# A relational graph layer on one core: row fetches with counters of their own, narrower first halves, later place transposes

## The chip, the cores and the metric

The kernel runs on one core of a Trainium2 chip. A core has five engines that run side by side, each with its own list of instructions in a fixed order, and that wait for one another through semaphores: TensorE (PE), which multiplies matrices and keeps its results in PSUM; VectorE (DVE) and ScalarE (ACT) for elementwise work; GpSimd (POOL), which here issues gathers; and SyncE (SP), which issues transfers. ACT issues transfers too. The metric is the device time of one execution in microseconds (us). The profile is that of one more execution.

## The reference

There are N = 12,500 nodes with 256 features each and E = 212,500 edges, sorted by destination; the last edge of each node is its loop to itself. Each edge has one of 8 types. What is computed:

```python
h = maximum(layernorm(x), 0)
hx = einsum('ni,rio->rno', h, weight)              # 8 weights of 256 x 256
agg = segment_sum(hx[edge_type, src], dst)         # sum over the edges into each node
out = x + agg * 0.5**0.5 + h_bias + (h @ loop_weight) * 0.5**0.5
```

All of it is float32. The kernel sums first and multiplies later: for each node and type it sums the rows h[src] of the edges, and multiplies the eight sums by the eight weights.

## The kernel before

**Units and tiles.** The sorted edge list is cut into 792 units. A unit holds up to 256 edges without their loops, as two tiles of 128 edges; there are 1583 tiles, numbered t. For a tile the kernel needs the 128 rows h[src], one to a partition (`msg`), and a one-hot matrix `oh` that says for each edge which column (destination within the unit's window of 22 nodes, times 8 types) it goes to. PE multiplies the two (`edge_sums`, line 883): the message rows are the stationary operand, in two halves of 128 features, and the one-hots move. One such product is two instructions in float32, so a tile is four pairs of weight load and matmul. A unit's second half of slots is multiplied first, over 22 x 8 = 176 columns; its first half (odd t) over `REACH[0][1]` x 8 = 16 x 8 = 128 columns, up to block 6, in which both take 176. DVE then adds the unit's sums to a ring of columns in SBUF at an offset that it has loaded into a register (`add_sums`, line 897); four PSUM banks take turns.

**Groups.** 128 nodes are a group; there are 98. When the last unit that can touch a group has been added, its 18 products with the weights (line 1070, 36 instructions of 256 columns) are queued and spread over the tiles that follow, from `ready` to `until`. `finish` (line 1082) adds the result to x and stores four groups at a time. It then prepares the ring slot six groups on: `begin` transposes that group's own rows (line 924) and writes its loop edges through eight DVE instructions (line 942). At every fourth group it queues `find_types`: a search on PE (line 975), a chain of DVE steps (lines 981 to 994) and a spread on PE (line 1002).

**Order of work.** The whole program is written in one order by the loop over t: at step t it issues the gather of tile t + 64, up to `FETCH` row fetches on SP and as many on ACT, one-hots a few tiles ahead, the tile's matmuls, and small jobs. Jobs that need the one shared PSUM bank `pt` go through `shared`: a first part on PE, then DVE parts two tiles later. A job may not run before the tile at which it was queued plus `wait`, nor while another one is active. Each engine then takes its instructions in that order and waits where data is missing.

**Blocks.** 128 units are a block. Its edge lists are prepared 232 tiles ahead in small steps: loads on SP, eight small loads of spans by ACT (line 363), and from 20 tiles later one DVE step per tile (lines 416 to 660). These compact the lists, transpose them on PE (line 372) and end in `places`: positions in the ring are computed on DVE (line 659) and transposed on PE (line 664). `verdict` checks after the last block (line 679) that every edge found a column; all engines read its flag, and a general path follows only if one did not.

**Messages.** A gather is one indirect transfer of 128 rows by POOL (line 818). `msgs` holds 66 tiles, so a tile's buffer is free once PE has read the tile 66 before it. From block 1 on, every 36th tile (t % 36 = 35, tiles 287 to 1511, 35 of them) is not gathered: SP and ACT fetch its rows one by one. `gather` queues four chunks of 32 rows, in turn for SP and ACT, from 8 tiles later. A chunk (`load_sources`) first loads 32 row numbers into registers (line 825), then issues 32 transfers of 1 KB each (line 831):

```python
for i, v in reversed(list(enumerate(vals))):
    fetches[engine].insert(0, (0, lambda i=i, v=v: queue.dma_start(
        msg[t][r0 + i : r0 + i + 1, :].bitcast(U8),
        h32_bytes[:, bass.ds(v, D * 4)])))
```

The framework gives each transfer of SP and ACT one of eight semaphores in turn. The next transfer that gets the same semaphore waits for the one before, whichever of the two engines issued it, and PE waits for all eight before it reads a fetched tile.

Of the kernel before, what the change touches and what calls it, by code (L numbers as in the profile page):

```python
# [11 lines left out]
U8 = mybir.dt.uint8  # L12
# [6 lines left out]
SYNC_DEP = mybir.DependencyInfo(mybir.DependencyClass.Sync, mybir.DependencyReason.DATA)  # L19
DVE = mybir.EngineType.DVE  # L20
SP = mybir.EngineType.SP
ACT = mybir.EngineType.Activation

P = 128
# [15 lines left out]


WIN = 22
REACH = ((0, 16), (0, 22))

GROUP = 128

# [4 lines left out]
MSGS = 66  # L51
AHEAD = 64

SINGLE = 36
FETCH = 3
SOURCES = 32
HOLD = 8


QUAD = 4  # L60
# [8 lines left out]
SOON = 8  # L69
# [9 lines left out]

PREP = 232  # L80
LOADED = 20
SHARE = 1.15
OVERDUE = 24

# [143 lines left out]
def kernel(  # L228
# [11 lines left out]
    nc = tc.nc  # L240
# [9 lines left out]
    U = PAIR * P  # L250
# [42 lines left out]
    with ExitStack() as main:  # L293
# [30 lines left out]
        firsts, stops, loops, marked, typed, gidx, col = {}, {}, {}, {}, {}, {}, {}  # L324
        added, zeroed = {}, {}
        single, fetches = {}, {SP: [], ACT: []}
        state = {"h32": None}


# [37 lines left out]
        def turned(got, cols, to):  # L367

            def turn():
                for i in range(PAIR):  # L370
                    half = slice(i * P, (i + 1) * P)
                    nc.tensor.transpose(pt[:, half], got[cols][:, half], ident)  # L372

            return [lambda: shared(turn, [(2, lambda: nc.vector.tensor_copy(to(), pt[:, :U]))])]

        def work_tile(got, name, tag, dtype=F32):
            got[name] = ep.tile(
# [268 lines left out]
        def places(b, got):  # L646

            def wraps_():
                got["wrapped"] = small.tile([P, NK], F32, name="wrapped")
                nc.vector.tensor_scalar(  # L650
                    got["wrapped"], wraps, got["base"][:, 0:1], None, op0=ALU.is_lt)

            def turns():
                got["turns"] = small.tile([P, 1], F32, name="turns")
                nc.vector.tensor_reduce(got["turns"], got["wrapped"], AX.X, ALU.add)

            def position():
                got["pos"] = small.tile([P, 1], F32, name="pos")
                nc.vector.scalar_tensor_tensor(
                    got["pos"], got["turns"], float(-RING), got["base"][:, 0:1],  # L660
                    op0=ALU.mult, op1=ALU.add)

            def turn():
                nc.tensor.transpose(pt[0:1, :P], got["pos"], ident)

            def keep():
                place[b] = small.tile([1, P], I32, name="offs")
                nc.vector.tensor_copy(place[b], pt[0:1, :P])

            return [wraps_, turns, position, lambda: shared(turn, [(2, keep)])]  # L670

        def verdict(got):

            def count():
                got["count"] = small.tile([P, 1], F32, name="count")
                nc.vector.tensor_reduce(got["count"], counts, AX.X, ALU.add)

            def total():
                nc.tensor.matmul(pt[0:1, 0:1], got["count"], ones, start=True, stop=True)  # L679

            def differs():
                nc.vector.tensor_scalar(flag, pt[0:1, 0:1], float(E), None, op0=ALU.not_equal)

            def compare():
                shared(total, [(2, differs)])

            def load():
                state["general"] = nc.values_load(flag[0:1, 0:1], min_val=0, max_val=1)

            return [count, compare, load]  # L690
# [5 lines left out]
        def shared(first, then, ready=lambda: True, wait=0):  # L696

            if done["tile"] is None:
                first()
                for _, f in then:  # L700
                    f()
                return
            jobs.append((first, list(then), ready, done["tile"] + wait, done["step"]))
# [94 lines left out]
        def gather(t):  # L798
            if t % PAIR == 0:
                both = msgs.tile([P, PAIR, D], F32, name="msg")  # L800
                for i in range(PAIR):
                    msg[t + i] = both[:, i, :]
            if t % QUAD:
                kind[t] = kind[t - 1]
            else:
                kind[t] = "h" if state["h32"] is not None and t >= state["h32"] + LATE else "x"
            table = {"h": h32, "x": x}[kind[t]]
            b, i, u = place_of(t)
            if b and t % PAIR and kind[t] == "h" and t + AHEAD < NT:
                if t % SINGLE == SINGLE - 1:  # L810
                    for k, r in enumerate(range(0, P, SOURCES)):
                        engine = ACT if k % 2 else SP
                        fetches[engine].append((
                            done["tile"] + HOLD,
                            lambda r=r, engine=engine: load_sources(t, r, engine)))
                    return
            at = i * P + u
            nc.gpsimd.indirect_dma_start(  # L818
                out=msg[t], out_offset=None, in_=table[:, :],
                in_offset=bass.IndirectOffsetOnAxis(ap=gidx[b][:, at : at + 1], axis=0))  # L820

        def load_sources(t, r0, engine):

            b, _, u = place_of(t)
            _, vals = nc.values_load_multi_w_load_instructions(
                single[b][u : u + 1, r0 : r0 + SOURCES], engines=[engine],
                min_val=0, max_val=(N - 1) * D * 4,
                skip_runtime_bounds_check_because="clamped to the table where they are computed")
            queue = {SP: nc.sync, ACT: nc.scalar}[engine]
            for i, v in reversed(list(enumerate(vals))):  # L830
                fetches[engine].insert(0, (0, lambda i=i, v=v: queue.dma_start(
                    msg[t][r0 + i : r0 + i + 1, :].bitcast(U8),
                    h32_bytes[:, bass.ds(v, D * 4)])))

        def fetch(n):
            for list_ in fetches.values():
# [31 lines left out]
        def edge_sums(t):  # L868
            m, o = msg.pop(t), oh.pop(t)
            if t % PAIR == 0:  # L870
                bank = banks[t // PAIR % BANKS]
                sums["ps"] = bank[:, : KC * R * WIN].rearrange("p (c k) -> p c k", c=KC)
            ps = sums["ps"]
            i = t % PAIR
            width = R * (REACH[0][1] if i and t // (PAIR * P) < NB - 1 else WIN)
            end = t == NT - 1 or i == PAIR - 1
            free = added.get(t // PAIR - BANKS)
            if i == 0 and free is not None and latest["pe"] is not None:
                tc.add_manual_dep(latest["pe"], free.name, SYNC_DEP, reason="bank is free")
            if i == 0 and latest["pe"] is not None:  # L880
                tc.add_manual_dep(latest["pe"], made[t], SYNC_DEP, reason="one-hots are made")
            for c in range(KC):
                j = nc.tensor.matmul(  # L883
                    ps[:, c, :width], m[:, c * P : (c + 1) * P], o[:, :width],
                    start=(i == 0 and c == 0), stop=(end and c == KC - 1))
            latest["pe"] = j.ins
            return ps

        sums = {}
# [77 lines left out]
        def find_types(q):  # L967
# [37 lines left out]
                typed[q] = types.tile([P, XG * GROUP], BF16, name="types")  # L1005
                nc.vector.tensor_copy(typed[q], pt)

            shared(spread, [(2, types_of)], lambda: q in marked, wait=2)

        got = {}  # L1010

# [103 lines left out]
        with tc.manual_schedule():  # L1115
# [111 lines left out]
            for t in range(NT):  # L1227
# [57 lines left out]
                while waiting and (len(waiting) > LAG or t == NT - 1):  # L1285
                    u, ps = waiting.pop(0)
                    add_sums(u, ps)
                    while (next_group < plan.NG and plan.last[next_group] <= u
                           and (done["weights"] or (NT <= 400 and done["norm"] == len(pieces)))):
                        g = next_group  # L1290
                        while background and NT <= 400:
                            step()
                        until = PAIR * (plan.first[g + SLOTS] - 3) - REST if g + SLOTS < plan.NG else NT - 1
                        ready = t + max(0, min(DELAY, NT - 1 - t - 2 * DELAY))
                        until = max(ready, min(until, ready + int(GROUP / plan.rate * PAIR)))
                        if g >= plan.NG - SOON:
                            until = min(until, ready + DELAY)
                        if g and g % SLOTS == 0:
                            wrap(g)
                        work = [] if g else group_ahead(0)  # L1300
                        work += group_work(g)
                        if g + 1 < plan.NG:
                            work[-8:-8] = group_ahead(g + 1)
                        for c, f in work:
                            queue.append((ready, until, c, f))
                        next_group += 1
# [36 lines left out]
```

## Time and profile before

| | us |
|---|---|
| median of 3 runs (2461.66 to 2462.48) | 2462.18 |
| the profiled execution | 2461.46 |
| its span, first to last instruction | 2459.7 |
| PE busy with matmuls | 1914.6 (78%) |
| DVE busy | 1385.7 (56%) |
| POOL busy | 1474.6 (60%) |
| ACT busy (issues not counted) | 143.5 (6%) |

The page gives busy time by engine, the same in 40 slices of the span with the clock that PE was granted, and groups of instructions by source line with the mean duration of one and the idle time just before it. PE stands for matmuls, PEld for the weight loads that run beside them. A row of the waits says which engine's instruction waited for what: total us, times, longest. "issue" is idle time in which the profile shows nothing that was waited for; "remote" is a semaphore whose raiser it could not name. A line of the timeline has the start in us, the duration, the engine, the source line, the operation, and a count where several were merged. "ACTq" and "SPq" are issues of transfers by ACT and SP, which do not count as busy. A table of stretches gives for each the busy time and number of instructions of an engine, the granted clock and what the transfers moved.

### The profile page before, as it was taken

What the parts mean: (1) busy time and instruction counts of PE and PEld (TensorE: products, weight loads), DVE (VectorE), ACT (ScalarE), POOL (GpSimd) and SP (SyncE); (2) the same over time, 40 slices, a digit from 0 to 9 for tenths busy, and PEclk for the clock granted to TensorE, in tenths of its full rate; (3) what the DMA queues carried; (4) which work ended last, traced back from release to release, by engine and by line L of the source; (5) the groups of instructions that cost most, each with busy time, mean ns of one, the idle gap of its engine ahead of it and who ended that gap; (6) DMA issues with size and microseconds to landing.
All of it is one profiled execution on the core that took longest, in us unless ns stands there. A gap on an engine that the chain in (4) does not pass through costs nothing. (4 is left out here: it accounts for less than half of the span.)

```text
span 2459.7 us, 38134 instructions
## 1 busy us (share of the span) xinstructions
PE 1914.6 (78%) x10339; PEld 1679.8 (68%) x10339; DVE 1385.7 (56%) x3530; ACT 143.5 (6%) x267; POOL 1474.6 (60%) x1574
## 2 busy tenths in 40 slices
PE   0157888888888877888888788788888888878889
PEld 0146677777777767777777677677777677777788
DVE  3387735446754546755455765455765445765453
ACT  3474300000000000000000000000000000000000
POOL 7535666666666666666666666666666666666630
PEclk9558998989998999898999999999899999999999
DMA  6584433343333333333333333334333333333320
GB/s 203 165 295 132 124 93 116 90 125 106 101 114 106 100 116 109 103 107 97 117 107 106 116 106 99 108 99 123 108 99 114 109 96 108 117 99 117 110 73 13
DMA packets 155220, 279.46 MB, mean 114 GB/s; under 512 B 33679, under 2 KB 105464, under 8 KB 155000
## 3 DMA queue, kind: packets, MB, share of 16 engines
q0 software_dynamic: 74304, 203.00, 27.8%
q1 hardware_dynamic: 74616, 71.68, 9.3%
q10 hardware_dynamic: 6080, 2.31, 0.4%
q8 instruction: 82, 1.34, 0.2%
q14 instruction: 138, 1.13, 0.1%
HBM read 251.26 MB, written 25.60 MB: 113 GB/s over the span
## 5 line engine op out<-in xcount | busy, mean ns | idle before, releaser
L818 POOL DMA_INDIRECT msg<-h,gidx x1448 | 1377.8, 952 | 815.6 <-issue 354.3
L883 PE MATMUL ps<-oh,msg 128*128 128x176 f32 (+1 forms) x6332 | 1191.2, 315 | 326.7 <-issue 177.4
L883 PEld LDWEIGHTS ps<-oh,msg 128*128 128x128 f32 x6332 | 1079.1, 206 | 474.8 <-issue 283.8
L1070 PE MATMUL po<-w,acc 128*128 128x256 f32 x3136 | 945.6, 402 | 113.0 <-issue 102.5
L897 DVE TENSOR_TENSOR acc<-acc,ps 128x352 f32 x792 | 408.9, 516 | 700.1 <-remote 364.0
L1070 PEld LDWEIGHTS po<-w,acc 128*128 128x128 f32 x3136 | 564.5, 201 | 206.3 <-issue 166.2
L850 DVE TENSOR_TENSOR oh<-fixed,cols 128x704 f32<-128x704 f32 x397 | 349.0, 880 | 0.0
L942 DVE SCALAR_TENSOR_TENSOR acc<-types,pt 128x256 f32<-128x256 bf16 (+1 forms) x688 | 248.9, 412 | 105.2 <-remote 54.6
L818 POOL DMA_INDIRECT msg<-in_x_dram,gidx x100 | 94.8, 948 | 83.5 <-issue 46.4
L1070 PE MATMUL po<-wl,self_t 128*128 128x256 f32 x392 | 113.3, 408 | 13.9 <-issue 7.9
L1070 PEld LDWEIGHTS po<-wl,self_t 128*128 128x128 f32 x392 | 71.8, 204 | 26.7 <-issue 13.6
L1082 DVE TENSOR_TENSOR xr<-xr,po 128x256 f32<-128x256 f32 x98 | 40.5, 413 | 32.4 <-PE po L1070 14.7
L772 ACT ACTIVATE msg<-msg,e_shift,e_rstd 128x256 f32<-128x256 f32 x100 | 51.8, 589 | 21.5 <-DVE e_shift L769 10.2
L772 ACT ACTIVATE xt<-xt,n_shift,n_rstd 128x256 f32<-128x256 f32 x98 | 50.9, 589 | 21.6 <-DVE e_stats L760 7.0
L924 PE MATMUL pt<-ident,hr 128*128 128x128 f32 x196 | 41.8, 292 | 12.7 <-issue 9.4
L1083 DVE TENSOR_TENSOR xr<-xr,po 128x256 f32<-128x256 f32 x98 | 41.2, 421 | 4.4 <-DVE xr L1082 1.1
L929 DVE COPY self_t<-pt 128x256 f32<-128x256 f32 x98 | 40.8, 416 | 1.8 <-remote 1.6
L398 DVE TENSOR_SCALAR moves<-fixed 128x271 int32<-128x271 int32 (+1 forms) x90 | 40.6, 451 | 2.1 <-issue 0.7
L400 DVE COPY_PREDICATED fixed<-moves,fixed 128x311 int32<-128x311 int32 (+14 forms) x90 | 38.0, 422 | 3.1
L924 PEld LDWEIGHTS pt<-ident,hr 128*128 128x128 f32 x196 | 26.6, 151 | 17.2 <-issue 12.0
L760 DVE BATCH_NORM_STATS2 e_stats<-msg 128x6 f32<-128x256 f32 x100 | 34.9, 411 | 0.0
L760 DVE BATCH_NORM_STATS2 n_stats<-xt 128x6 f32<-128x256 f32 x98 | 34.4, 412 | 0.7 <-issue 0.7
(243 smaller groups left out, 338.4 us busy)
## 6 DMA issues: line engine op xcount, KB each, us to landing
msg<-h SPq DMA_DIRECT2D x2240, 1.0 KB
msg<-h ACTq DMA_DIRECT2D x2240, 1.0 KB
msg<-h,gidx POOLq DMA_INDIRECT x1448
xt<-in_x_dram SPq DMA_DIRECT2D x24, 512.0 KB
h<-xt SPq DMA_DIRECT2D x24, 512.0 KB
xr<-in_x_dram SPq DMA_DIRECT2D x24, 512.0 KB
hr<-h SPq DMA_DIRECT2D x24, 512.0 KB
out_dram<-xr SPq DMA_DIRECT2D x24, 512.0 KB
```

Source lines behind the costliest of these rows:

```text
L398: nc.vector.tensor_single_scalar(m, packed[:, :n], 1 << (bit + k), op=ALU.bitwise_and)
L760: nc.vector.bn_stats(stats[:n, j, :], rows_[j])
L772: nc.scalar.activation(rows_[j], rows_[j], AF.Relu, bias=shift[:n, j : j + 1], scale=rstd[:n, j : j + 1])
L818: nc.gpsimd.indirect_dma_start(out=msg[t], out_offset=None, in_=table[:, :], in_offset=bass.IndirectOffsetOnAxis(ap=gidx[b][:, at : at + 1 ...
L850: j = nc.vector.tensor_tensor(o[:, k : k + v, :i, :], iota_f.unsqueeze(1).unsqueeze(1).to_broadcast([P, v, i, C]), of.unsqueeze(3).to_broa ...
L883: j = nc.tensor.matmul(ps[:, c, :width], m[:, c * P : (c + 1) * P], o[:, :width], start=(i == 0 and c == 0), stop=(end and c == KC - 1))
L897: i = nc.vector.tensor_tensor(a, a, ps, op=ALU.add)
L924: nc.tensor.transpose(pst[:, c, :n], rows_[:n, c * P : (c + 1) * P], ident[:n, :n])
L929: nc.vector.tensor_copy(got["self", g][:, :, :n], pst[:, :, :n])
L942: i = nc.vector.scalar_tensor_tensor(acc[:, :, r, s0 : s0 + n], of, float(r + 1), pst[:, :, :n], op0=ALU.is_equal, op1=ALU.mult)
L1070: i = nc.tensor.matmul(got["out", g][:n], lhs, rhs, start=(r == R and c == 0), stop=(r == R - 1 and c == KC - 1))
L1083: nc.vector.tensor_add(rows_[:n, k, :], rows_[:n, k, :], got["out", g][:n])
```

## The change

Four things change together.

- Rows: one tile in 28 is fetched row by row (t % 28 = 27, tiles 279 to 1511), in eight chunks of 16 rows. Chunks 0, 3 and 6 (48 rows) go to SP and the other five (80 rows) to ACT, and up to four items per engine are issued at each step. Each row's transfer raises one of four counters, in turn by fetched tile, instead of one of the eight shared semaphores. PE waits for the tile's counter once. The first row of a chunk waits until PE has read the tile that used the counter before.
- The first half of a unit covers 13 nodes, 104 columns, in place of 16 and 128.
- The transposes of places and of the verdict wait four tiles after being queued. The spread of types waits eight in place of two.
- For the last eight groups the products are ready one tile after the sums in place of six.

```diff
-REACH = ((0, 16), (0, 22))
+REACH = ((0, 13), (0, 22))
...
-SINGLE = 36
-FETCH = 3
-SOURCES = 32
+SINGLE = 28
+FETCH = 4
+SOURCES = 16
+BY_SP = (0, 3, 6)
 HOLD = 8
+COUNTERS = 4
...
+SETTLE = 4
...
+        counters = [tc.alloc_semaphore(f"rows{i}") for i in range(COUNTERS)]
+        fetched, summed = {}, {}
...
-            return [wraps_, turns, position, lambda: shared(turn, [(2, keep)])]
+            return [wraps_, turns, position, lambda: shared(turn, [(2, keep)], wait=SETTLE)]
...
-                shared(total, [(2, differs)])
+                shared(total, [(2, differs)], wait=SETTLE)
...
+                    fetched[t] = len(fetched)
                     for k, r in enumerate(range(0, P, SOURCES)):
-                        engine = ACT if k % 2 else SP
+                        engine = SP if k in BY_SP else ACT
...
+            k = fetched[t]
+
+            def fetch_row(i, v):
+                j = queue.dma_start(
+                    msg[t][r0 + i : r0 + i + 1, :].bitcast(U8), h32_bytes[:, bass.ds(v, D * 4)])
+                j.then_inc(counters[k % COUNTERS], 16)
+                tc.no_tile_sem_insts.add(j.ins.name)
+                tc.add_to_no_dep_group(f"rows{t}", j.ins)
+                if i == 0 and k >= COUNTERS:
+                    tc.add_manual_dep(
+                        j.ins, summed[k - COUNTERS], SYNC_DEP, reason="counter is at rest")
+
             for i, v in reversed(list(enumerate(vals))):
-                fetches[engine].insert(0, (0, lambda i=i, v=v: queue.dma_start(
-                    msg[t][r0 + i : r0 + i + 1, :].bitcast(U8),
-                    h32_bytes[:, bass.ds(v, D * 4)])))
+                fetches[engine].insert(0, (0, lambda i=i, v=v: fetch_row(i, v)))
...
+            if t in fetched:
+                k = fetched[t]
+                j = nc.tensor.wait_ge(counters[k % COUNTERS], 16 * P * (k // COUNTERS + 1))
+                tc.declare_fence(j.ins, group=f"rows{t}")
             for c in range(KC):
                 j = nc.tensor.matmul(
...
             latest["pe"] = j.ins
+            if t in fetched:
+                summed[fetched[t]] = j.ins.name
...
-            shared(spread, [(2, types_of)], lambda: q in marked, wait=2)
+            shared(spread, [(2, types_of)], lambda: q in marked, wait=2 * SETTLE)
...
                         ready = t + max(0, min(DELAY, NT - 1 - t - 2 * DELAY))
+                        if g >= plan.NG - SOON:
+                            ready = min(ready, t + 1)
```

More of the change, by code (lines that the diff above doesn't have):

```diff
@@ L372, in turn @@
                     nc.tensor.transpose(pt[:, half], got[cols][:, half], ident)
-            return [lambda: shared(turn, [(2, lambda: nc.vector.tensor_copy(to(), pt[:, :U]))])]
+            return [lambda: shared(
+                turn, [(2, lambda: nc.vector.tensor_copy(to(), pt[:, :U]))])]
         def work_tile(got, name, tag, dtype=F32):
```

## The prediction

> **What bounds the kernel now.** I read the page's busy rows and slices first, then the waits, then the groups by form, then short stretches of the timeline. The profiled execution took 2461.46 us, 0.7 below the median of the runs (2462.18); its span is 2459.7, so 1.8 lie around it. All sums below are against 2461.5. About 0.2% (5 us) is what a measurement of this kernel can tell from no change.
>
> ```profile
> PE 1914.6 (78%) x10339; PEld 1679.8 (68%) x10339; DVE 1385.7 (56%) x3530; ACT 143.5 (6%) x267; POOL 1474.6 (60%) x1574
> PE   0157888888888877888888788788888888878889
> PEclk9558998989998999898999999999899999999999
> ```
> PE is the busiest engine in every slice after the first three, at a granted clock of about 0.93.
>
> ```profile
> POOL msg L818 <- issue: 400.7, 1190, 7.2
> POOL msg L818 <- remote: 260.6, 171, 2.8
> PE ps L883 <- issue: 177.4, 290, 2.4
> POOL msg L818 <- PE ps L883: 134.1, 113, 3.4
> PE po L1070 <- issue: 110.4, 157, 2.9
> PE pt L1002 <- DVE diagonal L994: 17.6, 9, 3.8
> PE pt L1002 <- DVE kinds L991: 10.9, 4, 3.5
> PE pt L664 <- DVE pos L659: 7.4, 2, 5.0
> PE ps L883 <- DMA msg<-h,gidx: 7.3, 10, 1.1
> PE ps L883 <- DMA msg<-h: 2.8, 2, 1.8
> ```
> These are rows of the waits. POOL waits some 395 us (remote and PE) for message buffers that PE has not read yet, while PE waits 7 us for gathers and 3 us for fetched rows. So PE sets the pace and the gathers follow. PE's largest idle part, 288 us of "issue", is waiting for nothing shown.
>
> ```profile
> 460.00:2333.00 1873.00, 947.16 (x5087) 859.60 (x5086) 0.93 0.36 108
> ```
> ```profile
> 2000.35 29.82 ACTq L831 DMA_DIRECT2D msg<-h  x64
> 1100.10 34.89 ACTq L831 DMA_DIRECT2D msg<-h  x64
> L825 ACTq TENSOR_LOAD <-single x70: 811/2258/3020, 343.0 to 2278.5; - x70
> ```
> The first is line 883 by stretches: 5087 instructions of four per tile are 1272 tiles in 1873 us, 1.473 us a tile. The next two are ACT's timeline: 64 single rows and the second of two register loads of one tile take 30 to 35 us. One tile in 36 is fetched, so ACT has 53 us for it, and it does wait for buffers between tiles. The last is line 825: a load of 32 row numbers takes 2.26 us.
>
> **Narrower first halves.** 768 tiles of four matmuls go from 128 columns to 104.
>
> ```profile
> L883 PE MATMUL ps<-oh,msg 128*128 128x176 f32 x3260 | 702.1, 335 | 154.2 <-issue 89.6 <-remote 44.5 <-ACT msg L772 14.6
> L883 PE MATMUL ps<-oh,msg 128*128 128x128 f32 x3072 | 538.1, 293 | 172.4 <-issue 87.8 <-DVE acc L897 77.5 <-DMA msg<-h,gidx 4.2
> ```
> ```profile
> 344.47 0.19 PEld L1070 LDWEIGHTS po<-wl,self_t 128*128 128x128 f32 x1
> 344.49 0.46 PE L1070 MATMUL po<-wl,self_t 128*128 128x256 f32 x1
> 2370.09 0.19 PEld L883 LDWEIGHTS ps<-oh,msg 128*128 128x128 f32 x1
> 2370.16 0.31 PE L883 MATMUL ps<-oh,msg 128*128 128x128 f32 x1
> ```
> At full clock, starts of matmuls of one form lie 149 ns apart at 176 columns, 216 at 256, and 109 to 112 at 128: 0.833 ns a column and 2.5. By that alone 104 columns start 89 ns apart. But each has its own load of 128x128 weights, and the timeline shows what that needs. At 344.49 a matmul follows short ones, starts 23 ns after its load began, and lasts 462 ns where its kind lasts 379: 83 longer, so the weights were ready about 106 ns after the load began. At 2370.16 one starts 70 ns after its load and lasts 310 instead of 275: again 105. The next load there starts 109 ns after the one before, not at the matmul's start. So a load of full f32 weights takes about 107 ns and the next begins only when the first is in use: four loads cost 4 x 109 whatever the columns are. Bounds: 0, and 3072 x 20 ns = 61 us. I take 0, the case that the rows show directly (at best 1 to 2 ns each, 3 to 6 us). DVE's one-hots keep 176 columns and cost the same.
>
> The Trainium skill, "TensorE: Matmul & The Clock Gate", section "LDWEIGHTS (loading the stationary operand)", has a weight load cost columns / 1.2 ns, 107 ns for 128 columns. By that rule, the trace agrees: nothing is gained. [...]
>
> **Place transposes four tiles later.** L664 follows its DVE step directly, and PE idles 7.4 us (2 times) plus 1.0 and 0.5 for L650 and L655. Four tiles are 5.9 us, longer than the longest wait (5.0). Gain 8.9 at most, 0 at least; I take 9, since DVE is 56% busy and nothing else asks for these places for tens of tiles. The other use of the constant, eight tiles for the spread of types, changes nothing: in the written order the search for types is queued behind the eight own writes of its group and runs 8 tiles after queueing, its result is due 2 later and the spread 2 after that, 12 tiles, so a floor of 8 is passed already. The 28.5 us at L1002 stay. The verdict's transpose moves too, at 0.3 us of idle.
>
> **Gathers.** Fetched tiles go from 35 to 45 (tiles 279 to 1511), gathers from 1548 to 1538. POOL spends 0.95 + 0.30 us each, but it waits for PE; 12.5 us less work there is worth 0. If PE's issue stalls belonged to the gathers (288 / 1548 = 0.19 us each) it were 2; I take 1.
>
> **Counters.** PE's four semaphore instructions ahead of a fetched tile become one wait: 35 x 4 to 45, each some 0.1 us and partly beside running matmuls; -2, bounds 0 and -10. On ACT the eight semaphores that SP and ACT share no longer hold a row back. On each queue they cost ACT about 85 us over 2240 rows in this trace (251 gaps that end 0.02 us after the landing waited for).
>
> **Last eight groups.** Their products start five tiles earlier. In 2360 to 2450 us PE is all but never idle, so order is worth nothing there; a product could wait half a us for DVE's sum: 0 to +4, I take 0.
>
> **What the row fetches cost ACT.** This decides. ACT now issues 80 rows for each of 45 tiles, 3600 instead of 2240; SP 2160 instead of 2240. A chunk is 16 rows. From this trace, per chunk on ACT: 0.26 us from the last row to the register load; the load, 1.33 (one value takes 0.47, 32 take 2.26; DVE's 16 at L862 take 1.10); 0.13 to the first row; 0.60 to the second; then 14 gaps. Half of all gaps are 0.327 us, the floor; the mean, with gaps that end on a shared semaphore set to the floor, is 0.45, because ACT, SP and PE all show issue steps of 0.7 and 1.4 us, and because rows stand behind SP's 512 KB issues (gaps of about 2.1). So 0.26 + 1.33 + 0.13 + 0.60 + 14 x 0.45 = 8.6, and 43.0 us a tile. There are 28 x 1.473 = 41.2 us for it, 41.0 with the small gains. At the floor alone it were 34.5; at 0.49 (the worst fifth of this trace, 900 to 1300 us) 45.9. SP needs 3 chunks of about 11 us in the same time and stays ahead.
>
> ACT therefore falls behind by about 2 us a fetched tile, after a lead of some 53 us (a buffer is free 98 us before use; 98 - 43 - 2). It can issue the first row when PE has read tile 213 (445.9 us) and did so 6 us after such a point: 452. Then 45 x 43.0 = 1935; 19 for ACT's loads of spans (line 363), in the same queue; 2 until the last row lands; then PE reads tile 1511 and finishes as today, 2459.7 - 2363.7 = 96 us later; 2 around the span. Sum 452 + 1935 + 19 + 2 + 96 + 2 = 2506 us. Queued behind ACT's rows are only those span loads; late, they make DVE wait at line 421, but that is inside the same sum. With PE alone the time would be 2461.5 - 9 - 1 - 2 = 2449.5. The larger of the two holds.
>
> **Rivals.**
> - *ACT keeps up.* For it: half the gaps are at the floor, and without the shared semaphores ACT no longer waits on SP's. Against: with these gaps taken out the mean is still 0.45. It needs a chunk under 8.35 us (gaps below 0.43): then 2449, a gain of 0.5%, from the place transposes. This is the case on the other side.
> - *The 104 columns pay.* PE needs 61 us less: 2388 if ACT also needs under 40.3 us a tile, else ACT's time. Against: the two weight loads above.
> - *ACT's stalls grow with its load.* If the issue steps come with the number of issues (29% more rows): gaps near 0.49, 45.9 us a tile, 571 + 2066 = 2637.
>
> **How the numbers follow.** ACT binds and slower: 0.60, around 2506 (own range 2467 to 2580, gaps 0.43 to 0.475); stalls grow: 0.05; within 0.2%, ACT just at the edge: 0.08; ACT keeps up: 0.22 (2436 to 2456); columns pay: 0.05. Faster 0.27, same 0.08, slower 0.65. The range 2436 to 2580 leaves out the columns (0.05), most of the growing stalls and the tail above: under 0.2.
>
> **What would show it.** ACT's queue on line 831 without a pause from about 700 us on, with 80 rows in about 43 us; new PE waits on line 883 for DMA msg<-h of some 50 us, once per 28 tiles, all in the second half; L664 waits gone, L1002 waits still near 28; form 128x104 with starts still 109 apart. I am wrong if ACT still pauses for buffers between tiles at 2000 us, or if 104-column starts lie near 89 ns.

## The result and the profile after

The changed kernel takes 2470.05 us (median of 11 runs, 2468.01 to 2472.59) where the kernel before takes 2462.41 in the same comparison: a ratio of 1.0027, 95% interval 1.002 to 1.0035. A second comparison gave 1.0025 (1.0016 to 1.0034). So it is slower, by about 6.5 us; forecast were 44.

The page of the changed kernel, profiled execution 2472.6 us (span 2470.9): busy times, PE's row of slices, its granted clock.

```profile
PE 1913.4 (77%) x10339; PEld 1689.2 (68%) x10339; DVE 1387.2 (56%) x3530; ACT 143.6 (6%) x267; POOL 1470.2 (60%) x1564
PE   1157888778888887878788788878878788888899
PEclk9558989999999999999999999999899999988899
```

PE sets the pace as before. The rows of its waits, and of POOL's (total us, times, longest):

```profile
POOL msg L825 <- issue: 396.8, 1189, 7.1
POOL msg L825 <- remote: 262.3, 177, 2.5
PE ps L904 <- issue: 197.0, 295, 1.7
POOL msg L825 <- PE ps L904: 148.1, 112, 2.8
PE po L1093 <- issue: 103.4, 152, 2.9
PE pt L1025 <- DVE diagonal L1017: 16.2, 8, 4.7
PE pt L1025 <- issue: 12.3, 7, 3.9
PE ps L904 <- DMA msg<-h,gidx: 8.4, 11, 1.1
PE pt L1025 <- DVE kinds L1014: 4.9, 1, 4.9
```

What is missing here decides the case: there is no row "PE ps L904 <- DMA msg<-h". PE waits for no fetched row at all, where the forecast had some 50 us of such a wait. POOL still waits 410 us for buffers. The spread of types (L1025) waits 33.4 us where it waited 31.1, as forecast. PE's two large issue rows stand at 300 us against 288.

Line 904 over the same stretch that the prediction used, in the view of stretches (PE busy and instructions, PEld busy and instructions, clock, DMA share, GB/s):

```profile
460.00:2333.00 1873.00, 928.67 (x5061) 857.43 (x5061) 0.93 0.37 108
```

5061 instructions are 1265 tiles where there were 1272: 1.480 us a tile against 1.473. The loss is spread thin over the stretch in which rows are fetched; tile by tile the two traces drift apart by 5.5 us between tiles 279 and 1511. The rest of this one execution's distance lies in the last 72 tiles, 86.5 us against 82.0, at a clock of 0.96 against 1.00; a run below shows that the edit there costs nothing.

Then ACT, in the view of lines 832 and 840 (durations are min/median/max in ns, then first and last start):

```profile
L832 ACTq TENSOR_LOAD <-single x225: 3/1323/2597, 344.5 to 2305.3; - x113
L840 ACTq DMA_DIRECT2D msg<-h x3600: 2/228/877, 450.4 to 2312.2; - x190
L840 SPq DMA_DIRECT2D msg<-h x2160: 3/198/1362, 450.5 to 2310.0; - x197
```

Over all 45 tiles ACT takes 38.3 us from the first to the last of its 80 rows (a tenth of them over 42.3), and the step to the next tile's first row needs 1.7 more (0.26 to the register load, 1.32 for it, 0.13 behind it): 40.0 us. PE gives it 28 x 1.48 = 41.4. The rest is waiting: in the trace ACT stands still behind the load, until PE has read the tile whose buffer the row goes to, ahead of 23 of the 44 later tiles, for some 63 us in all (4.9 us up to 1980 us, 2.3 up to 2024). ACT issues its last row 38 to 61 us ahead of PE's use of it, from the first fetched tile to the last. It keeps up, with 3% to spare. SP takes 31.3 us for its 48 rows and stays 49 to 67 us ahead.

### The profile page after: what moved, and what is told of

It is laid out like the page before. It is cut to its first block, busy times and chain, and to the rows that moved or that the text cites. A ratio compares the mean times of both kernels' runs of the same rounds, so it can differ in the third digit from the quotient of the medians.

```text
span 2470.9 us, 40674 instructions
## 1 busy us (share of the span) xinstructions
PE 1913.4 (77%) x10339; PEld 1689.2 (68%) x10339; DVE 1387.2 (56%) x3530; ACT 143.6 (6%) x267; POOL 1470.2 (60%) x1564
## 4 chain that ended last, share of the span: by engine, by line
PE 60%; issue 15%; DVE 12%; another core or an unknown queue 6%; POOL 2%; DMA 2%; ACT 1%; DVEq 0%; SPq 0%; ACTq 0%; POOLq 0%
PE ps L904 30%; PE po L1093 28%; POOL msg L825 2%; DVE acc L920 2%; DVE oh L867 1%; DVE acc L965 1%; DVE e_stats L766 1%; PE pt L947 1%; DVE n_stats L766 1%; DMA msg<-h,gidx 1%; DVE moves L404 1%; DMA w<-in_L_gnn_weight_dram 1%; DVE fixed L406 0%; DVE e_mv L768 0%
## 5 line engine op out<-in xcount | busy, mean ns | idle before, releaser
L904 PE MATMUL ps<-oh,msg 128*128 128x176 f32 (+1 forms) x6332 | 1173.9, 312 | 348.1 <-issue 197.0
L904 PEld LDWEIGHTS ps<-oh,msg 128*128 128x128 f32 x6332 | 1082.6, 206 | 490.1 <-issue 254.0
L1093 PE MATMUL po<-w,acc 128*128 128x256 f32 x3136 | 959.8, 408 | 101.5 <-issue 93.4
L1093 PEld LDWEIGHTS po<-w,acc 128*128 128x128 f32 x3136 | 571.4, 203 | 194.1 <-issue 162.2
L947 PE MATMUL pt<-ident,hr 128*128 128x128 f32 x196 | 41.4, 290 | 17.5 <-issue 13.0
L1025 PE MATMUL pt<-diagonal,ones_b 128*128 128x512 bf16 x22 | 9.3, 424 | 33.4 <-DVE diagonal L1017 16.2
```

The source lines that it names most:

```text
L904: j = nc.tensor.matmul(ps[:, c, :width], m[:, c * P : (c + 1) * P], o[:, :width], start=(i == 0 and c == 0), stop=(end and c == KC - 1))
L947: nc.tensor.transpose(pst[:, c, :n], rows_[:n, c * P : (c + 1) * P], ident[:n, :n])
L1093: i = nc.tensor.matmul(got["out", g][:n], lhs, rhs, start=(r == R and c == 0), stop=(r == R - 1 and c == KC - 1))
```

## The experiments

Ratios are against the kernel before in the same round of runs, with 95% intervals. In most rounds the kernel before takes 2461 to 2487 us; in one, with four experiments, it takes 1982, and these are told apart. Rounds of both kinds are on record under the same chip number, so nothing here shows what differs between them.

### Which of the four parts costs

One part of the change at a time, each put into the kernel before. Narrower first halves:

```diff
-REACH = ((0, 16), (0, 22))
+REACH = ((0, 13), (0, 22))
```

> Only the first halves of units go from 128 to 104 columns. Theory A (weight loads set the pitch): four loads of about 109 ns a tile whatever the columns are, so 0, at most 3 to 6 us better, and the starts at 104 columns alternate between about 89 and 112 ns as they do in the changed kernel, with the time caught up where the next load is waited for. Theory B (columns set the pitch, and something else in the changed kernel ate the gain): 3072 x 20 ns = 61 us better. Theory C (the narrower form costs PE idle time): the row of PE's waits on line 883 for issue grows from 177 towards the 197 of the changed kernel, and the time by up to 8 us.

Later transposes (`wait=SETTLE` at the two jobs, 2 * SETTLE at the spread):

```diff
-            return [wraps_, turns, position, lambda: shared(turn, [(2, keep)])]
+            return [wraps_, turns, position, lambda: shared(turn, [(2, keep)], wait=SETTLE)]
```

> Only the transposes of places and of the verdict wait four tiles, and the spread of types eight. As predicted: the 8.9 us of PE's waits at line 664 go, the waits at the spread stay near 30 us, and the time falls by 9. Rival: the idle time was not worth its length, because PE caught up behind it or another wait takes its place: 0, within 2 us. If this part alone is slower, the later transposes put something else off.

The last eight groups:

```diff
+                        if g >= plan.NG - SOON:
+                            ready = min(ready, t + 1)
```

> Only the products of the last eight groups start one tile after the sums. As predicted: 0, bounds 0 to +4. Theory S (from the changed kernel's last 72 tiles, which took 86.5 us where they took 82.0): +4 to +5, all after tile 1511. Rival: those 4.5 us belong to the lower clock in the last slices of that execution, then 0.

The fetched rows, that is all that the diff shows of SINGLE, FETCH, SOURCES, BY_SP and the counters:

```diff
-SINGLE = 36
+SINGLE = 28
...
+                j.then_inc(counters[k % COUNTERS], 16)
```

> All of the row fetches' changes (counters of their own, one tile in 28, 80 rows by ACT and 48 by SP, chunks of 16, up to four items a step), nothing else. The theory that was predicted (ACT at 43.0 us a fetched tile binds) asks for about 2515. The theory from the changed kernel's trace (ACT at about 40.0 us a tile keeps up with 41.3): no wait of PE for fetched rows, and what is left is what the rows do to PE's issue stalls. If they carry the difference, +6 to +16 us (7.6 seen, and 9 more if the later transposes gain what was predicted); if the rows are free, -3 to +1.

The kernel before has a median of 2462.56 us in this round.

| part alone | median us | ratio |
|---|---|---|
| 104 columns | 2460.99 | 0.9997 (0.9989 to 1.0006) |
| later transposes | 2461.81 | 0.9997 (0.9988 to 1.0006) |
| last eight groups | 2461.10 | 0.9996 (0.9988 to 1.0005) |
| rows | 2468.49 | 1.0029 (1.0017 to 1.0040) |

The rows carry all of it, +7 us, and the other three are nothing. A gain of 9 us from the later transposes would be a ratio of 0.9963 and is excluded, although the waits at the place transposes did shrink as forecast. Of the 8.9 us this kernel's trace has 3.9 left:

```profile
PE pt L665 <- DVE self_t L930: 2.8, 2, 2.3
PE pt L665 <- DVE pos L660: 1.1, 1, 1.1
```

Nor is there a cost of the early products: theory S falls.

That the columns bring nothing can be read without any time of a run. The timeline of PE in a stretch without stalls, in the kernel before and in the changed one:

```profile
211.34 0.61 PE L883 MATMUL ps<-oh,msg 128*128 128x128 f32 x4
211.79 0.60 PE L1070 MATMUL po<-w,acc 128*128 128x256 f32 x2
212.22 0.61 PE L883 MATMUL ps<-oh,msg 128*128 128x176 f32 x3
```

```profile
212.79 0.59 PE L904 MATMUL ps<-oh,msg 128*128 128x104 f32 x4
213.21 0.62 PE L1093 MATMUL po<-w,acc 128*128 128x256 f32 x2
213.67 0.61 PE L904 MATMUL ps<-oh,msg 128*128 128x176 f32 x3
```

Both take 0.88 us from the first to the third line. In ns, the median over some 350 such places: the four matmuls of a first half with their way to the next instruction take 444 at 128 columns and 424 at 104, because the first of them starts its successor 89 ns later instead of 109. But the first of the two products behind then waits for its own weights: its successor starts 238 ns later instead of 218. From the first half to the tile behind it are 878 ns in both (some 245 of the 350 places have no stall). Where another tile follows directly, 596 and 596.

### How much a fetched row costs, and at which end

```diff
-SINGLE = 36
+SINGLE = 1 << 20
```

> The kernel before without any row fetches: all 1583 tiles are gathered. Theory D (each row that is issued costs PE a little, 6 us for 1280 more rows, 4.6 ns a row): 4480 rows fewer, 15 to 25 us faster if POOL keeps pace, since it waits 395 us for buffers and has 35 x 1.25 = 44 us more work. Rival P (the gathers cost PE more than the rows, or POOL's work is not all hidden): slower, by up to 44 us, with new waits of PE for the gathers. Rival N: within 2 us, and the rows are not where the 6 us come from.

2437.56 us, ratio 0.9905 (0.9889 to 0.9920): 23.4 us faster. This version beats both kernels here, with nothing but gathers. The rows of its waits, and its busy line:

```profile
PE 1933.0 (79%) x10339; PEld 1690.3 (69%) x10339; DVE 1385.4 (57%) x3530; ACT 143.6 (6%) x267; POOL 1511.7 (62%) x1609
POOL msg L818 <- remote: 212.6, 116, 2.9
PE ps L883 <- issue: 152.6, 268, 1.7
PE po L1070 <- issue: 85.6, 151, 1.7
POOL msg L818 <- PE ps L883: 83.8, 63, 2.3
```

The 35 tiles cost POOL 37 us of busy time more, and POOL still waits 296 us for buffers. PE's two issue rows fall from 288 to 238 us, 50 less. PE's busy time rises by 18 while its granted clock falls (0.906 in the mean of the runs before, 0.894 in these), and of the 50 about half is left: 26 us between the two spans. Theory D holds: 23.4 us over 4480 rows are 5.2 ns a row, and the expectation had 4.6. This is a net price: each 128 rows fewer are also one gather more.

The same in the changed kernel (SINGLE = 1 << 20 in place of 28), and the fetches of one engine alone, at one tile in 72, in the kernel that has only the rows' part of the change:

> The changed kernel without any row fetches. If the fetched rows carry all of the difference, it loses 5760 x 5.2 ns = 30 us against the changed kernel and comes to the time of the kernel before without fetches: 2437.6, within 2 us, since the other three parts are worth 0 each. Rival (the later transposes and narrower halves pay once PE is not held by rows): 2428 to 2434.

```diff
-SINGLE = 28
-BY_SP = (0, 3, 6)
+SINGLE = 72
+BY_SP = ()
```

> The kernel before with counters, one tile in 72 fetched (18 tiles, 2304 rows), all of its rows by ACT, chunks of 16. Theory D (each row costs PE 5.2 ns, whichever engine issues it): 2437.6 + 12 = 2449.6. Theory A (in the traces slow gaps of ACT's rows fall together with PE's stalls, 0.26 of their time against 0.14 in fast gaps, and SP's do not, 0.20 against 0.19; so ACT's rows alone cost, about 10 ns each): about 2460.

(and BY_SP = tuple(range(8)), HOLD = 3 for SP)

> The same with all rows by SP, queued five tiles sooner so that SP has time. Theory D: 2449.6, as with ACT. Theory A (only ACT's rows cost): 2437.6. If SP falls behind, PE waits at the fetched tiles show it, and are taken off first.

In this round the kernel before took 2486.81, so ratios are compared. The changed kernel without fetches: 0.9897 (0.9882 to 0.9913), that is -1.3% from 1.0027, 32 us. Of the rival's gain, in which the other three parts pay once the rows are gone, nothing is seen: the kernel before with all tiles gathered stands at 0.9895 in the same round (`loads_only`, told below). A gain of more than some 5 us is excluded. Rows by ACT: 0.9954 (0.9941 to 0.9968). Rows by SP: 0.9942 (0.9929 to 0.9956). Neither trace has a wait of PE for fetched rows.

| rows | compared with | difference | ns a row |
|---|---|---|---|
| +1280 | before | +0.0029, 7.1 us | 5.6 |
| -4480 | before | -0.0095, 23.4 us | 5.2 |
| -5760 | changed | -0.0130, 32 us | 5.6 |
| +2304 by ACT | 0.9896, all gathered | +0.0058, 14.4 us | 6.3 |
| +2304 by SP | 0.9896, all gathered | +0.0046, 11.4 us | 5.0 |

(0.9896 is the mean of the two runs of that round in which all tiles are gathered.) One price fits five comparisons, and the engine that issues makes no difference that these intervals can tell (about 2 ns on the last two rows). Theory A, that only ACT's rows cost, asked for 0.9896 with SP and is excluded. All five trade 128 rows for one gather, so 0.7 us a fetched tile would fit them as well as a price a row; no run tells the two apart.

PE's idle time for "issue", all lines together, goes the same way: 269 to 288 us in the traces of four kernels in which all tiles are gathered, 292 to 322 in six with one tile in 36 fetched, 314 to 349 in three with one in 28. One trace alone can't carry this, since traces of kernels of equal time differ by 30 us.

### What the counters and the split do

> One tile in 36 as before, 64 rows each, chunks of 32; only the counters are new. Predicted: -2, bounds 0 and -10, from PE's shorter wait for a fetched tile. Theory C (the counter itself costs, as more tight issue on the queues): +3 or more. Theory D (the number of rows costs): -2 to 0, and ACT's rows of one tile run through faster than before.

> One tile in 36 as before, with the counters, the split of 80 and 48 rows and chunks of 16. Theory D (the number of rows): within 2 us of the kernel before. Rival U (the split or the smaller chunks, with eight register loads a tile in place of four): +3 to +6.

```diff
-SINGLE = 36
+SINGLE = 28
```

> The kernel before with one tile in 28 fetched, over the eight shared semaphores, 64 rows each, chunks of 32. SP took 47.7 us and ACT some 35 us and more a tile of 53 us; now there are 41.3. Theory Q (the shared queues bind): SP needs 6 us a tile more than there is, 45 x 47.7 = 2146 us from about 450 on, and the time is 452 + 2146 + 96 + 2 = about 2700, with PE waiting for rows at line 883. Rival: part of the 47.7 us was waiting for others, and the queues keep up: within 10 us of the kernel before, with +6 if the number of rows costs.

Counters alone: 1.0002 (0.9993 to 1.0011). With the split and the smaller chunks: 1.0004 (0.9995 to 1.0013). Both are nothing at one tile in 36. One tile in 28 over the shared semaphores, though, in the kernel before: 2561.38 us, 1.0406 (1.0391 to 1.0421). Here PE does wait for fetched rows:

```profile
PE ps L883 <- DMA msg<-h: 176.3, 26, 11.0
PE ps L883 <- issue: 138.6, 213, 5.8
```

and SP for transfers of rows, its own or ACT's, which the view doesn't tell apart:

```profile
SPq L831 <- DMA msg<-h: 140.1, 207, 11.0
```

SP is the late one: from the thirteenth fetched tile on, in all but a few tiles, it issues its last row only 0 to 3 us ahead of PE's need. So the queues do bind at one tile in 28, though by 100 us and not the 240 of theory Q: pressed, SP takes 40.5 us from its first row to its last and not 47.7, so part of the latter was waiting. What makes one tile in 28 possible is the counters together with the split of 80 and 48 rows in chunks of 16; no run has one without the other at that rate. With the counters alone, at one tile in 36, SP's 64 rows still take 42.2 us from the first to the last, more than the 41.3 that one tile in 28 leaves, where its 48 rows take 31.3. The price of the rows is what makes it not worth having.

The traces also show what the counters do to ACT's gaps. Mean gap from the second row of a chunk to its last on ACT, and the shares of these gaps from 0.36 to 0.5 us and above 2 us:

| kernel | mean us | 0.36 to 0.5 | above 2 |
|---|---|---|---|
| before | 0.502 | 13.6% | 1.7% |
| counters alone | 0.431 | 5.0% | 0.3% |
| counters, 80 and 48, chunks of 16 | 0.410 | 4.5% | 0.2% |
| changed | 0.410 | 4.9% | 0.3% |

The drop is not mainly in the many short ones. Of the 91 ns between the top line of the table and the bottom one, gaps of 0.36 to 0.5 us make up 6, those of 0.5 to 1.3 us 44 and those above 2 us 29.

### Which part of a row it is

> All tiles are gathered, and for one in 36 the register loads of the row numbers are made too (80 numbers by ACT, 48 by SP, chunks of 16), but no rows are fetched. Theory R (the rows' transfers cost PE): 2437.6, within 2 us. Theory L (the loads of 4480 numbers cost): up to 2461. A value between says how the 24 us split.

This run did not test it: nothing used the numbers, and the trace has none of these loads. It is a second run with all tiles gathered, 0.9895 (0.9880 to 0.9910). So one transfer of 64 bytes a chunk was added, which keeps the loads:

```diff
+            queue.dma_start(
+                unused[engine][:, :].bitcast(U8), h32_bytes[:, bass.ds(vals[0], 64)])
```

> All tiles are gathered; for one in 36 SP and ACT load the 128 row numbers in chunks of 16 and issue one transfer of 64 bytes a chunk, so that the loads stay in the program: 280 loads and 280 transfers. If the register loads of the rows cost PE: near 1.000 of the kernel before. If the transfers do: 0.990 to 0.992, as without fetches.

> All tiles are gathered; for one in 36 SP and ACT also load the 128 row numbers (chunks of 16, 48 and 80) and issue 128 transfers of 32 bytes instead of 1 KB, into a tile that nobody reads. So 4480 transfers, register loads and address moves as before, with 1/32 of the bytes. The kernel without fetches stands at 0.9905 of the kernel before. If the transfers cost PE by their number: 0.998 to 1.002. If they cost by their bytes or by writing the message buffers: 0.990 to 0.992.

> All tiles are gathered; for one in 36 ACT runs 256 copies of one element, as many instructions as the fetches had (two for each row), with no transfers. If the instructions of another engine cost PE (their stream has to be brought in like PE's): near 1.000 of the kernel before. If not: 0.990 to 0.992.

> The kernel before with the matmuls of the first halves over 32 columns instead of 128. It leaves out the sums of the other columns. If the weight loads alone set the pitch (about 109 ns for four in a row), the time is within 6 us of the kernel before. If columns set it: 3072 x 80 ns = 246 us faster, or 3072 x 20 = 61 us if there is a floor near 90 ns.

These four ran in the round in which the kernel before takes 1981.76 us, and there the bound is another. The waits of the kernel with 32 columns:

```profile
POOL msg L818 <- issue: 371.6, 1208, 2.7
PEld ps L885 <- DMA msg<-h,gidx: 182.7, 267, 3.3
PE ps L885 <- DMA msg<-h,gidx: 97.3, 145, 2.9
POOL msg L818 <- PE ps L885: 57.0, 187, 0.3
```

PE's issue rows, 288 us in the other rounds, are gone (0.5 us at the products, none at the tiles). PE waits for gathers instead, and POOL hardly for PE. A gather saved from POOL is worth something here: with all tiles gathered the time is 2024.72 with the loads kept (1.0213, 1.0199 to 1.0227) and 2023.26 with ACT's small copies (1.0210, 1.0196 to 1.0224), 42 us more for 35 gathers of 1.25 us. So these runs say nothing about PE's price for a row. The transfers of 32 bytes took 2078.74 us (1.0485, 1.0468 to 1.0502), for a reason of their own: ACT's 80 transfers of a tile, here over the shared semaphores, take 49 us from the first to the last and put the loads of spans off that stand behind them in its queue, and DVE waits:

```profile
DVE from__24941 L428 <- DMA spans<-in_dst_dram: 74.4, 1, 74.4
DVE from__19897 L428 <- DMA spans<-in_dst_dram: 72.1, 1, 72.1
DVE from__14870 L428 <- DMA spans<-in_dst_dram: 61.1, 1, 61.1
```

That is the consequence which the prediction named for a late ACT.

32 columns: 1983.2 us, 1.0006 (0.9997 to 1.0015). With the gathers as the bound a shorter PE would not show in that time, so the trace is read instead, at the places used above: the four matmuls take 363 ns to the next instruction, the first product 299, and the way to the tile behind is 878 again. 128, 104 or 32 columns give the same 878 ns.

Two more runs were for what this left open.

> The changed kernel once more. Where the kernel before takes about 2462 or 2487 us and PE idles some 290 us for issue: 1.0027 again (1.002 to 1.0035), as 1280 more rows cost PE 6 to 7 us. Where the kernel before takes about 1982 us (there PE has next to no such idle time, waits 97 to 280 us for gathers, and without fetches the time is 2.1% longer, 42 us for 35 tiles): ten more fetched tiles take ten more gathers of 1.25 us off POOL, 12 us or 0.994, as long as ACT keeps up; it has 28 x 1.23 = 34.4 us a fetched tile there and needs 33.8 at the shortest gaps, so if it falls behind the time is 1.00 or more.

> All tiles gathered, 280 loads of 16 row numbers and 280 transfers of 64 bytes. Where the kernel before takes about 2462 or 2487 us: 0.990 to 0.992 if the rows' transfers are what costs PE, near 1.000 if the register loads are. Where it takes about 1982: 1.021 again.

Both ran where the kernel before takes 2461.81. The changed kernel gave 1.0025, told above. The loads alone: 2441.12 us, 0.9919 (0.9905 to 0.9933), as without fetches within the intervals. That these loads are there, the view of line 831 shows; the other two lines are of this kernel's waits:

```profile
L831 ACTq TENSOR_LOAD <-single x175: 1192/1237/1320, 342.6 to 2220.7; - x175
L831 SPq TENSOR_LOAD <-single x105: 333/1221/2826, 397.3 to 2213.3; - x105
PE ps L891 <- issue: 174.3, 314, 1.7
PE po L1080 <- issue: 86.7, 147, 2.2
```

So some 3 of the 24 us, by the intervals at most 9, belong to the register loads with their 280 small transfers; the rest belongs to the address moves and row transfers that follow them, or to something else that comes with a fetched tile. Whether by their number, their bytes or their instructions stays open, because the two runs that would tell ran in the round of 1982 us.

This kernel ran in both kinds of round, unchanged: 2441.12 us here, 2024.72 there. Its busy lines, here and there:

```profile
PE 1937.4 (79%) x10339; PEld 1690.0 (69%) x10339; DVE 1384.3 (57%) x3530; ACT 143.6 (6%) x267; POOL 1507.2 (62%) x1609
PE 1787.4 (88%) x10339; PEld 1545.7 (76%) x10339; DVE 1394.2 (69%) x3530; ACT 142.4 (7%) x267; POOL 1510.7 (75%) x1609
```

DVE, ACT and POOL are as busy in both. PE is busy 150 us less there, at a granted clock of 0.97 against 0.90, and idle 262 us less: 288 us of "issue" are gone. Why is open, and so is what the changed kernel does in such a round, where it saves ten gathers but leaves ACT less time.

## Why the prediction was wrong

**The step that failed first is "then 14 gaps", at "the mean, with gaps that end on a shared semaphore set to the floor, is 0.45".** All other terms of the chunk came out: load 1.32 (1.33), first to second row 0.58 (0.60), last row to load 0.26 (0.26); the load's end to the first row 0.14 (0.13). The gap was 0.41, and with it the step "ACT therefore falls behind by about 2 us a fetched tile" fell: ACT waited for buffers, at 2000 us too, which the prediction had named as a sign of being wrong. A chunk costs 0.26 + 1.32 + 0.14 + 0.58 + 14 x 0.41 = 8.0 us and not 8.6, a tile 40.0 and not 43.0. The edge lay at 41.0, so an error of 7% in one term turned a bound of 2506 us into slack. The correction made for the shared semaphores took out only the gaps that end just after the landing waited for. Redone on the same trace, that gives 0.45. If every gap is set to the floor in which a landing waited for falls anywhere (330 of 2100 in place of some 266), it gives 0.42, close to the 0.43 measured with the counters alone. The gaps above 2 us, which the prediction put down to SP's 512 KB issues, went from 1.7% to 0.3% with these issues still there. The mechanism, that a queue too late for its tile makes PE wait, is sound: one tile in 28 over the shared queues is 4% slower, with such waits, though there it was SP that came late. As for the range, by the prediction's own sum gaps of 0.43 and 0.475 give 2448 and 2589 us and not 2467 and 2580.

**The rival that came nearest, "ACT keeps up", missed by some 20 us.** Of these 9 are the place transposes, below, and most of the rest is a term that the sum for PE doesn't have: what the rows cost PE. The only term near it is "If PE's issue stalls belonged to the gathers [...] it were 2; I take 1", and in rounds of 2461 to 2487 us its sign was wrong. A tile moved from one gather to 128 row transfers costs PE 128 x 5.2 = 0.7 us; ten tiles are 6.7 us.

**Place transposes: "Gain 8.9 at most, 0 at least; I take 9."** It was 0 (-3 to +1.5 us). The waits went; the time did not. Why is not settled.

**Counters on PE**, -2 forecast: +0.5 measured (-1.7 to +2.7). **Last eight groups**, 0: 0. **Spread of types**, unchanged: 31.1 and 33.4 us. **SP ahead**: it is, by 49 us and more. **Waits at the places**: 1.1 us left on DVE in the changed kernel.

**Narrower halves, 0 forecast**: 0 measured, for the reason given. The Trainium skill, "TensorE: Matmul & The Clock Gate", section "LDWEIGHTS (loading the stationary operand)", lets 128 columns of weights load in 107 ns (columns / 1.2); by that rule, the trace agrees, with 109 to 112 ns from start to start at 128 columns and 878 ns from tile to tile whatever the moving columns are. The prediction was careless in one place: it said that 104-column starts near 89 ns would prove it wrong. One of four starts does lie at 89, and the wait for a later load takes the 20 ns back.

With the terms as measured the sum closes. ACT keeps up, so PE alone counts: the prediction's 2449.5, plus 9 for the transposes, plus 2 for the counters, plus 1 + 6.7 for the gathers, is 2468.2; measured were 2470.05 and 2467.57.

## What to carry to other kernels

When a forecast rests on one engine being 5% too slow, the term with the widest spread decides the sign: give the case in which it is fast enough the weight that this spread asks for, and check each small credit in it as hard as the main one. Moving work to idle queues is not free for the engine that sets the pace: the kernel with the moved work taken out altogether is the first run to make. Here it beat both kernels where they take 2461 us or more, and in the round of 1982 us it lost to the kernel before by 2%. A shorter matmul under weight loads that set the pitch gives its time back at a later load, as the 20 ns here, so measure to the start of the next tile and not to the next instruction.

## What the runs showed of the hardware

Fetching a tile by 128 transfers of 1 KB, issued by ACT or SP, in place of one gather costs PE some 0.7 us (5 to 6 ns a row) in rounds in which the kernel takes 2461 to 2487 us, without a wait on those rows in the profile; PE's "issue" idle time goes with it, from about 280 us in traces without fetched rows to about 310 and 330 with one tile in 36 and in 28. With 50 us less of that idle time PE was granted a clock of 0.894 instead of 0.906, was busy 18 us longer with the same work, and the span fell by 26. That less idle time is what lowers the clock isn't shown: one tile in 28 over the shared queues left PE 115 us more idle than before, with a clock of 0.883. From the start of four f32 matmuls, each with a 128x128 weight load of its own, over the two products behind them to the next tile it is 878 ns, with 128, 104 or 32 moving columns. And the same kernel took 1982 us in one round and 2461 to 2487 in others. In the first the issue idle time is absent, the gathers are the bound and a fetched tile is worth 1.2 us; the sign of moving rows off POOL is different in the two.
